# A four-stage gated network on one core: x transposed on TensorE instead of loaded a second time, rows and exponentials on ScalarE, and one list of steps ahead of the routed tiles

## The chip, the cores and the metric

The kernel runs on one core of one Trainium2 chip. The metric is the device time of one execution in microseconds, given as the median of several runs. The engines are called as the profile calls them: PE (TensorE, the matrix engine, with PEld for its weight loads), DVE (VectorE), ACT (ScalarE), POOL (GpSimd) and SP (SyncE, which here only issues transfers, DMAs). Each engine works through its own list of instructions in order, and waits on semaphores where an instruction needs what another engine or a transfer has not finished.

## The reference, cut to what matters

The input x has 4 sequences of 512 tokens with 512 features, 2048 tokens in all. Two layers follow, each an attention part and a feed-forward part, each part added to x through a gate:

```python
x = x + tanh(g_xattn[0]) * L0_xattn(layernorm(x), ctx, desc_router, W_q, b_q, itok)
x = x + tanh(g_ffn[0])   * L0_ffn(layernorm(x), gate_w, bias, experts, shared)
x = x + tanh(g_xattn[1]) * L1_xattn(layernorm(x), ctx, ctx)
x = x + tanh(g_ffn[1])   * L1_ffn(layernorm(x), router_w, experts, shared)

# L0_xattn: 64 sets; each token may see 4 of them (itok), takes the best 2
scores = (ln @ W_q.T + b_q) @ desc_router.T / sqrt(512)
scores = where(mask, scores, -inf)
weights = softmax(top 2 of scores)          # one exp of a difference
out = weights @ ctx                         # 64 rows of 512 per sequence

# L0_ffn: 32 experts, the best 6 for each token, at most 192 tokens per expert
s = sqrt(softplus(h @ gate_w.T))
idx = top 6 of (s + bias);  w = 1.5 * s[idx] / sum(s[idx])
pos = running count of tokens per expert
y = sum of w * down(silu(h @ w_gate) * (h @ w_up)) + shared(h)
```

The change lies in the first two parts: from the load of x up to the point where the first tile of tokens routed to an expert goes through PE. I call this stretch the head. Layer 1 and the routed tiles of layer 0 are not changed.

## The kernel before

**Tiles.** x is kept in SBUF as 16 tiles `xs[t]` of 128 tokens by 512 features. They are handled in four groups of four tiles, `GROUPS[g]`: tile g of each of the four sequences. `lnT[g]` holds a group transposed, features on partitions (128 x 4 x 512). The head works on three parts of the groups for the attention (`PARTS`: group 0, group 1, groups 2 and 3 together; index u) and on two pairs of groups for the feed-forward part (index p: groups 0 and 1, groups 2 and 3).

**Loads.** SP issues them in the order of the code: the descriptor matrix, the four tiles of `w_q`, some small vectors, then per two groups the transposed x from DRAM (`xT`, 1 MB for each group, L133) and the tiles of x (256 KB each, L135). So x is read twice, once in each layout. Then come the weights of the shared expert and of the first two routed experts (L558, L559).

**The head's steps, before.**
- The mask of allowed sets is built by 16 small DVE operations (L296, L298), and `bm` from it (L301). PE multiplies the descriptors with `w_q` (`pm`), ACT and DVE take the row means off (`mrow`), PE transposes the product (`pmt`), and ACT copies it to `mT` (L330).
- `score1(p)`: PE multiplies `mT` with `lnT` of two groups (`pss`, L362), ACT copies (`sT`), PE transposes back (`pst`, L370). The scores of pair 0 serve u = 0 and u = 1.
- `look1(u)`: mean and variance of each x tile on DVE (L354, L355).
- `pick1(u)`: DVE only. It computes the inverse standard deviation by a bit trick and Newton steps (`rsqrt`), scales and masks the scores (L384, L389), finds the best two, and computes the exponential of their difference by a polynomial (`exp_parts`, L235 to L244, 13 operations), which gives the weights `wa`.
- `mix1(u)`: PE transposes `wa` (`pw`), ACT copies (`wT`), PE multiplies with ctx (`po`, L429), DVE adds the result to x and sums the rows (L430); then ACT sums the squares of x less its mean (L440).
- `norm2(p)` turns sums into scale and shift on DVE. `turn2(p)` computes the eight normalised tiles h of the pair on DVE (L470), stores each to `h_dram`, and has it transposed on PE (`transposed`, L256) and copied into `lnT` by ACT (L257). So from here `lnT` holds h.
- `logits2(p)`: router logits by PE (`pl`, L480), copied, transposed (`plt`), copied to `lg`.
- `gate2(p)`: DVE only, from `lg` to the six chosen experts (`sel2`), the running rows (`rows2`) and the weights `wts`, which SP stores beside h (L552). It begins at L505 with a polynomial exponential over 128 x 256.
- `shared0(g, ..., True)` for groups 0 and 1: the shared expert, as matmuls on PE (`pg0s`, `pu0s`, L577), Silu and a scaling on ACT, a product and a clip on POOL (L587, L588), and the down projection with x added (`po0s`, L596, L598).
- At the end the counts: running sums of `rows2` on DVE (L655 to L658), `ptot`, `pcnt` and `ppos` on PE, `counts` stored to `cnt_dram` (L670), the look-up rows `look2` on DVE (L686). Then POOL looks up counts (`found`, L761), DVE turns them into token numbers, POOL fetches the tokens' rows of h (`xb`, L783), and PE starts on the first routed tile (`ptb`, then `gu`, L801).

**What sets the order.** In the head, PE, DVE and ACT keep the order in which the code issues their instructions (`manual_schedule`). The calls are written out one by one after `run` is defined; several steps are Python generators, of which a call of `next` issues one piece. Behind the routed tiles' own loop the order comes from the string `ORDER`, a list of such steps. PSUM is shared: the pool `ps_t` has two buffers (tag "pt") for all transposes, the pool `ps` two for each of the tags "g", "u" and "o". The work pool has nine row buffers (tag "row").

## Time and profile before

| | |
|---|---|
| median of 3 runs | 1096.97 us (1096.78 to 1097.93) |
| the profiled execution's own time | 1097.25 us |
| its span, first to last instruction | 1095.5 us |
| busy in the span: PE | 1004.9 us, 92% |
| DVE | 466.5 us, 43% |
| ACT | 211.5 us, 19% |
| POOL | 376.1 us, 34% |
| mean granted PE clock | 0.961 of full |
| HBM read | 206.16 MB |

The page gives the busy time of each engine and then the span in 40 equal slices of 27.4 us: a digit is the busy share of an engine in tenths, and the row PEclk gives the clock that PE was granted, in tenths of full. A line of the timeline has the start in us, the duration in us, the engine, the line of the code, the operation, the tile written and the tile read, and in brackets how long the engine had been idle before and what released it. A line of the table by stretches has the busy time of each engine in a stretch with the number of its instructions. The duration of a group (x16 and the like) runs from its first start to its last end.

### The profile page before, as it was taken

The page shows a single profiled execution, that of the slowest core. Times are in us where ns is not written, and L with a number is a line of the kernel's source. Part 1 is how long each engine was busy: PE and PEld are TensorE (multiplying, and loading weights), DVE is VectorE, ACT ScalarE, POOL GpSimd, SP SyncE. Part 2 cuts the span into 40 slices and gives each one's busy share as a digit, 9 for nine tenths or more (in the row PEclk, how much of TensorE's full clock was granted, in tenths as well). Part 3 has the DMA queues.
Part 4 walks back from the last instruction along what each step waited for, and adds up shares of the span by engine and source line. Part 5 has one row for each costly group of instructions (what it writes and reads, how often), then busy time and mean ns, then how long its engine had stood idle before and what let it go on. Part 6 is the DMA issues. An engine that isn't in the chain of part 4 may idle for free. (4 is left out here: it accounts for less than half of the span.)

```text
span 1095.5 us, 11070 instructions
## 1 busy us (share of the span) xinstructions
PE 1004.9 (92%) x3334; PEld 491.7 (45%) x3334; DVE 466.5 (43%) x1244; ACT 211.5 (19%) x461; POOL 376.1 (34%) x414
## 2 busy tenths in 40 slices
PE   5569889999999999989779888999999999999998
PEld 2134344444444444434345433655555555544443
DVE  5989946232222232267788452122222222218111
ACT  1144111222222222113344300211111111110000
POOL 2001142234333222177562564445544554300000
PEclk8679999999999999999879899999999999999999
DMA  8622046778788777767463205427453734438111
GB/s 315 246 77 78 7 131 215 250 262 284 254 280 275 279 278 260 253 187 218 147 213 116 59 1 237 164 76 243 129 160 107 257 110 156 157 109 303 39 38 38
DMA packets 88381, 191.94 MB, mean 175 GB/s; under 512 B 24638, under 2 KB 41950, under 8 KB 81920
## 3 DMA queue, kind: packets, MB, share of 16 engines
q1 hardware_dynamic: 59664, 114.46, 29.8%
q0 software_dynamic: 28656, 76.76, 22.9%
q8 instruction: 27, 0.44, 0.2%
q14 instruction: 34, 0.28, 0.1%
HBM read 206.16 MB, written 35.57 MB: 221 GB/s over the span
## 5 line engine op out<-in xcount | busy, mean ns | idle before, releaser
L801 PE MATMUL gu<-wbuf,xbT 128*128 128x512 f32 (+1 forms) x512 | 174.0, 596 | 1.0 <-issue 0.7
L967 POOL DMA_INDIRECT yk<-y_dram,rows_of x76 | 84.1, 1106 | 83.9 <-DVE it0s L590 34.6
L783 POOL DMA_INDIRECT xb<-h_dram,get x48 | 48.0, 1000 | 166.5 <-issue 98.8
L808 DVE SCALAR_TENSOR_TENSOR sgb<-gu,xb,sgb 128x256 f32<-128x256 f32 (+1 forms) x64 | 30.9, 484 | 160.5 <-ACT sgb L806 121.3
L1458 PE MATMUL por<-wbuf,itr 128*128 128x512 f32 (+1 forms) x216 | 98.7, 592 | 0.0
L801 PEld LDWEIGHTS gu<-wbuf,xbT 128*128 128x128 f32 (+1 forms) x512 | 63.1, 163 | 78.0 <-issue 76.9
L1438 PE MATMUL pgr<-wbuf,xrT 128*128 128x352 f32 x288 | 91.6, 461 | 5.4 <-DMA wbuf<-in_wgu_dram,wrow 4.7
L1441 DVE SCALAR_TENSOR_TENSOR sgr<-pur,slots,sgr 128x352 f32<-128x352 f32 x36 | 21.0, 584 | 169.6 <-PE pur L1438 118.3
L826 PE MATMUL pob<-wbuf,itb 128*128 128x512 f32 (+1 forms) x256 | 91.2, 599 | 0.0
L1438 PE MATMUL pur<-wbuf,xrT 128*128 128x352 f32 x288 | 91.1, 459 | 0.0
L1227 PE MATMUL pg<-lnT,wbuf 128*128 128x512 f32 (+1 forms) x224 | 83.6, 561 | 0.1
L1227 PE MATMUL pu<-lnT,wbuf 128*128 128x512 f32 (+1 forms) x224 | 79.6, 532 | 0.0
L1461 POOL DMA_INDIRECT y_dram<-yr,put x36 | 36.8, 1021 | 123.9 <-DVE yr L1460 116.7
L1438 PEld LDWEIGHTS pur<-wbuf,xrT 128*128 128x128 f32 x288 | 54.7, 190 | 30.5
L1243 PE MATMUL po<-wbuf,it 128*128 128x512 f32 x128 | 61.3, 611 | 5.7 <-DVE pick L1322 3.8
L1438 PEld LDWEIGHTS pgr<-wbuf,xrT 128*128 128x128 f32 x288 | 51.9, 190 | 29.4 <-DVE yr L1460 3.8
L1458 PEld LDWEIGHTS por<-wbuf,itr 128*128 128x128 f32 (+1 forms) x216 | 41.0, 190 | 41.9 <-issue 34.9
L761 POOL DMA_INDIRECT found<-cnt_dram,look x48 | 48.5, 1010 | 25.7 <-issue 14.0
L1227 PEld LDWEIGHTS pg<-lnT,wbuf 128*128 128x128 f32 (+1 forms) x224 | 35.2, 184 | 42.7 <-issue 41.4
L1227 PEld LDWEIGHTS pu<-lnT,wbuf 128*128 128x128 f32 (+1 forms) x224 | 35.0, 175 | 40.9 <-issue 38.2
L831 DVE COPY y<-pob 128x512 f32<-128x512 f32 x48 | 33.2, 692 | 43.2 <-PE pob L826 31.6
L1460 DVE TENSOR_TENSOR yr<-por,half_db 128x512 f32<-128x512 f32 x36 | 24.9, 692 | 56.1 <-PE por L1458 50.8
(399 smaller groups left out, 1280.2 us busy)
## 6 DMA issues: line engine op xcount, KB each, us to landing
wbuf<-in_wgu_dram SPq DMA_DIRECT2D x32, 1024.0 KB
wbuf<-in_wd_dram SPq DMA_DIRECT2D x32, 512.0 KB
y_dram<-y SPq DMA_DIRECT2D x48, 256.0 KB
q<-rp SPq DMA_DIRECT2D x256, 32.0 KB
y<-y_dram SPq DMA_DIRECT2D x32, 256.0 KB
lnT<-in_xT_dram SPq DMA_DIRECT2D x4, 1024.0 KB
x<-in_x_dram SPq DMA_DIRECT2D x16, 256.0 KB
h_dram<-h SPq DMA_DIRECT2D x16, 256.0 KB
```

Source lines behind the costliest of these rows:

```text
L761: G.indirect_dma_start(out=found[k][:, j, :], out_offset=None, in_=cnt_dram[:, :], in_offset=bass.IndirectOffsetOnAxis(ap=look2[:, i : i + ...
L783: G.indirect_dma_start(out=rows0[i], out_offset=None, in_=h_dram[:, :], in_offset=bass.IndirectOffsetOnAxis(ap=get2[:, i : i + 1], axis=0) ...
L801: PE.matmul(gu[p_, :], lhsT=xbT[:, c, p_], rhs=weights[e][0][:, c, :], start=(c == 0), stop=(c == DC - 1),)
L808: V.scalar_tensor_tensor(sg[p_, :I0], gu[p_, I0:], xb[p_, D + e : D + e + 1], sg[p_, :I0], ALU.mult, ALU.mult)
L826: PE.matmul(po[p_, :], lhsT=it[:, ic, p_], rhs=weights[e][1][:, ic, :], start=(ic == 0), stop=(ic == I0 // P - 1),)
L831: V.tensor_copy(y, po)
L967: G.indirect_dma_start(out=yk, out_offset=None, in_=y_dram[:, :], in_offset=bass.IndirectOffsetOnAxis(ap=rows_of[:, t, k : k + 1], axis=0) ...
L1227: PE.matmul(p_[m, :n], lhsT=wgu[:, a, c, i], rhs=lnT[g][:, c, k], start=(c == 0), stop=(c == DC - 1))
L1243: PE.matmul(po, lhsT=it[:, ic, k * P : (k + 1) * P], rhs=wd[:, ic, :] if ic < 2 else wd2, start=(ic == 0), stop=(ic == 2),)
L1438: PE.matmul(p_, lhsT=xbT[:, c, :], rhs=wgu[:, a, c, :], start=(c == 0), stop=(c == DC - 1))
L1458: PE.matmul(po, lhsT=it[:ni, ic, :], rhs=wd[:ni, ic, :], start=(ic == 0), stop=(ic == 2))
L1461: d = G.indirect_dma_start(out=y4_dram[:, :], out_offset=bass.IndirectOffsetOnAxis(ap=put4[:, i : i + 1], axis=0), in_=yr, in_offset=None, ...
```

## The change

1. **x is no longer loaded transposed.** The argument `xT` and its four loads are gone. A new step `turn1(g)` has PE transpose each x tile (four 128 x 128 transposes into a buffer of `ps_t`) and ACT copy it into `lnT[g]`, 16 tiles in all.
2. **The mask** is built by POOL: four subtractions of 128 x 256, a product of 128 x 512 and one of 128 x 256, then one comparison with zero on DVE in place of 16 operations.
3. **The exponential in `pick1`** is one ACT activation (Exp), after a maximum on DVE. `gate2` keeps its polynomial.
4. **The h rows** are a step of their own, `rows2_(p)`. For pair 0 ACT computes them (Identity with scale and bias from tiles), for pair 1 DVE as before. `turn2(p)` only transposes.
5. **The counts** become a generator, `count2`, with the same instructions.
6. **One list of steps**, `FIRST_ORDER`, replaces the calls written out. Most steps yield in more places, so that they can be interleaved. A step "j" (`filler`) issues one matmul whose result nobody reads; the list has it twice: on PE it stands once ahead of `pw` of part 1 and once ahead of the last `po0s` of group 1.
7. Following the list, on PE the shared expert's first matmuls stand ahead of `pl` of pair 0, the second half's between the h transposes of pair 1, and group 1's among the `po0s` of group 0. On DVE, `norm2(1)` and seven of the eight h rows of pair 1 stand ahead of `gate2(0)`. On SP, the load of expert 2's first weights stands ahead of the second pair of `wts` stores. The lists of all engines behind the head are the same as before.

The core of the diff:

```diff
+FIRST_ORDER = """
+x1 x0*3 x1 x0 c1 x1*2 c1 c0*2 b0*2 c0*2 f0 x3 x2 x3 c1*2 f0*2 f1 c2 x3 m0*2 x2 x3 x2*2 b1 c2 j f1 m0 c2 f1 m1
+c2 m1 c2 b1 m1 c2*3 n0 h0 f2 h0 t0 h0*3 t0*2 f2 h0 t0*3 f2 m2 h0*2 m2 t0*2 m2*3 n1 h1 e0 h1 g0*2 t1*2 h1*3
+e0*2 h1 t1 h1 t1 r0 t1*3 e0 h1 t1 g1*2 r0 e1 r0 e1 r0 e0 r0 r1*4 o e0 e1 e0*2 e1 o*3 e1*3 r1 o j e1 o*2
+"""
...
-        if g % 2 == 0:
-            for h in range(2):
-                nc.sync.dma_start(out=lnT[g + h], in_=xT[g + h])
...
-    for g in range(TB):
-        V.tensor_scalar(mask[:, g, :], iota_f, itok_f[:, g, 0:1], None, ALU.is_equal)
-        for k in range(1, KSET):
-            V.scalar_tensor_tensor(
-                mask[:, g, :], iota_f, itok_f[:, g, k : k + 1], mask[:, g, :], ALU.is_equal, ALU.max
-            )
+    hit = chain[:, 1:5, :].rearrange("p a n -> p (a n)").rearrange("p (k g n) -> p k g n", k=KSET, n=N)
+    for k in range(KSET):
+        G.tensor_tensor(
+            hit[:, k], iota_f[:, None, :].to_broadcast([P, TB, N]),
+            itok_f[:, :, k : k + 1].to_broadcast([P, TB, N]), ALU.subtract,
+        )
+    G.tensor_tensor(hit[:, 0:2], hit[:, 0:2], hit[:, 2:4], ALU.mult)
+    G.tensor_tensor(mask, hit[:, 0], hit[:, 1], ALU.mult)
+    V.tensor_scalar(mask, mask, 0.0, None, ALU.is_equal)
...
+    def turn1(g):
+        for t in GROUPS[g]:
+            transposed(cols(t), xs[t], f"ptx{t}")
+            yield
...
-        exp_parts(r, d, m, q)
+        V.tensor_scalar(d, d, -87.0, None, ALU.max)
+        A.activation(r, d, AF.Exp)
+        yield
...
-    def turn2(p):
+    def rows2_(p):
         rs, nb = norms2[p]
         for j, t in enumerate(tiles2(p)):
-            h = work.tile([P, D], F32, name=f"h{t}", tag="row", bufs=NROW)
-            V.tensor_scalar(h, xs[t], rs[:, j : j + 1], nb[:, j : j + 1], ALU.mult, ALU.add)
+            h = hs[t] = work.tile([P, D], F32, name=f"h{t}", tag="row", bufs=NROW)
+            if p == 0:
+                A.activation(h, xs[t], AF.Identity, bias=nb[:, j : j + 1], scale=rs[:, j : j + 1])
+            else:
+                V.tensor_scalar(h, xs[t], rs[:, j : j + 1], nb[:, j : j + 1], ALU.mult, ALU.add)
             nc.sync.dma_start(out=h_dram[t * P : (t + 1) * P, :D], in_=h)
-            transposed(cols(t), h, f"pth{t}")
+            yield
+
+    def turn2(p):
+        for t in tiles2(p):
+            transposed(cols(t), hs.pop(t), f"pth{t}")
+            yield
...
+    def filler():
+        while True:
+            pj = ps_t.tile([P, DC, P], F32, name="pj", tag="pt")
+            PE.matmul(pj.rearrange("p c t -> p (c t)"), lhsT=ones, rhs=ctx_sb[:, 0, :], start=True, stop=True)
+            yield
...
+    ws0 = load_w0(0, wsgu0, wsd0)
+    does = {"o": count2()}
+    for p in range(2):
+        does |= {f"b{p}": score1(p), f"n{p}": norm2(p), f"h{p}": rows2_(p), f"t{p}": turn2(p), f"g{p}": logits2(p)}
+        does |= {f"r{p}": gate2(p), f"e{p}": shared0(p, *ws0, True)}
+        does |= {f"x{2 * p + a}": turn1(2 * p + a) for a in range(2)}
+    for u in range(len(PARTS)):
+        does |= {f"c{u}": look1(u), f"f{u}": pick1(u), f"m{u}": mix1(u)}
+    in_steps(FIRST_ORDER, does)
```

In the list a letter names a step and the digit its group, pair or part: x transposes of x, c statistics, b scores, f picks, m mixing, n norms, h rows, t transposes of h, g logits, r gate, e shared expert, o counts, j filler; "*3" issues three pieces.

## The prediction

> **What bounds the kernel now.** The page comes first: the sum of the busy shares, then the slices of 27.4 us.
>
> ```profile
> span 1095.5 us, 11070 instructions
> ...
> PE   5569889999999999989779888999999999999998
> ...
> DVE  5989946232222232267788452122222222218111
> ...
> PEclk8679999999999999999879899999999999999999
> ```
>
> PE is full nearly everywhere but in the first three slices, where DVE is full instead. The table by stretches splits there (columns: length, busy us of PE, PEld, DVE, ACT, POOL, then granted clock, DMA share, GB/s).
>
> ```profile
> 16.00:82.00 66.00, 38.73 (x136) 18.08 (x133) 56.98 (x239) 16.43 (x38) 0.00 (x0) 0.74 0.53 203
> 82.00:134.00 52.00, 45.48 (x137) 20.71 (x135) 48.50 (x159) 17.29 (x33) 8.77 (x8) 0.99 0.13 44
> 154.00:1095.00 941.00, 894.73 (x2988) 438.67 (x2988) 341.99 (x784) 172.10 (x380) 353.85 (x364) 0.98 0.55 181
> ```
>
> From 16 to 134 us DVE works 105.5 of 118 us, nearly all there is once gaps of 0.03 us between instructions are taken off; PE has slack and a clock of 0.74 in the first half. After 154 PE works 895 of 941 us, and the built instruction lists of all five engines are alike there in both kernels. So the change is worth what it moves the first routed tile (ptb, at 154.02), and that passes to the end. The timeline gives the stations on the way (start, duration, engine, line).
>
> ```profile
> 22.73 0.42 DVE L384 TENSOR_TENSOR s<-pst,rs_a 128x256 f32<-128x256 f32 x1 [0.72 <-PE pst L370]
> ...
> 82.26 0.42 DVE L505 SCALAR_TENSOR_TENSOR chain<-lg 128x256 f32<-128x256 f32 x1
> ...
> 133.22 0.69 DVE L658 TENSOR_TENSOR rows<-rows,upto 128x512 f32<-128x512 f32 x1
> ...
> 134.05 1.94 PE L661 MATMUL ptot<-rows,ones 128*128 128x480 f32 x2 [4.91 <-DVE rows L658]
> ...
> 143.54 1.64 POOL L761 DMA_INDIRECT found<-cnt_dram,look  x1 [11.35 <-DVE chain L704]
> ```
>
> The reader should see four stages: first scores (22.73), router logits of pair 0 taken up by DVE (82.26), running counts (end 133.85), first look-up (143.54). I carry the change through these, in the order of the built lists, with durations of this execution.
>
> **First scores: later.** Gone are four loads of 1 MB of xT. The first scores didn't wait for them long: pss started at 15.11, 0.05 after mT. In their place stand eight tile transposes and copies, behind a later mT. The mask moves from 16 DVE operations (4.65 us, from 6.89) to six on POOL: 128x256 lies between POOL's 0.44 us for 128x128 and its 1.30 for 128x512, so 0.70 each for five and 1.25 for one, with memsets between them 5.6 us from 6.8, end 12.4. DVE's list then has two mask operations, and behind them the mean of the score matrix, which PE needs: pmt starts at 13.85 instead of 12.56, and ends at 15.98. x tiles should be there: bytes flow at 400 GB/s from 9.1, and the first two groups with ctx are 2.5 MB, 6.3 us. Eight transposes follow, 0.89 us a tile at half clock (the eight h tiles from 61.73 took 6.86) and 0.66 at full clock, where ACT's 0.59 copy sets the pace.
>
> Here a rule speaks against the change. The rows:
>
> ```profile
> 60.00:64.00 4.00, 2.27 (x11) 2.08 (x12) 3.79 (x13) 0.88 (x2) 0.00 (x0) 0.50 0.40 148
> 64.00:67.00 3.00, 3.00 (x15) 2.35 (x13) 2.93 (x21) 2.03 (x4) 0.00 (x0) 0.50 1.02 383
> 67.00:68.00 1.00, 1.00 (x7) 0.76 (x6) 0.97 (x9) 0.61 (x2) 0.00 (x0) 0.66 0.92 346
> ```
>
> PE did only transposes from 61.73, and was granted full clock at about 67.7, 5.9 us after their start. The Trainium skill (TensorE: Matmul & The Clock Gate, Part 4: PE-mode transpose) says that transposes don't count as PE activity and full clock doesn't engage for them. By that rule all eight tiles run cold (7.1 us, 1.0 more than below), and the first 5 us of the score group too. That group took 6.24 us at 15.11, some 4.4 of them at half clock, so it is 4.1 at full clock; with 5 us at half clock it is 6.6, 2.5 more. Scores come 3.5 us later still, and the forecast below would be 1097.8. I go by the row: full clock about 5 us into dense work (the rises at 19.5, 36.9, 50.6 and 67.7 came 3.3 to 6.9 after), here at 19. Then: four tiles at 0.89 to about 19.4, four at 0.66 to 22.1, last copy 22.75, pss 4.1 to 26.9, sT 0.6, pst 0.7: DVE takes the scores at 28.2, 5.5 us later than now.
>
> **DVE's picks: that is won back.** Each pick loses 13 small operations (25.64 to 28.23, 2.6 us) for one maximum (0.2) and an Exp on ACT. No row shows this Exp; the nearest is the 128x2 activation at 9.46, 0.20 us, so 0.3 with both hand-overs: 2.1 us off, three times. The built list has no further table load for it. Bounds 0.2 to 0.6 each. Exp stands between copies on ACT, but those end 0.7 us earlier. Laid out: first pick 5.3 + two statistics 1.6 to 35.1; second scores 3.1, statistics and adds of four x tiles 3.55, rest of the second pick with statistics and the row means to 48.3; a wait of 0.6 for pw, wT, po; adds and statistics 6.2 and 0.5 of waiting for ACT's squares to 55.6; norm2 2.2 to 57.85; third pick 9.9: wa is there at 67.75, now 73.2. The second four-tile transposes of x use PE's idle time; their single free ps_t buffer (pst holds the other) costs them 1.4 us a tile, which nobody waits for. The two filler matmuls (0.45 us each) fall into waits of PE, for wa of the second pick and for xb at the end, where it rests 2.3 us now. The h rows of pair 0 leave DVE (3.74 us); on ACT they are priced by Square with a bias, 0.71 (no row has both scale and bias by pointer; by the Trainium skill, ScalarE: Activation LUTs, What ACT_TABLE_LOAD costs, each pointer adds 93 ns, so an estimate of 0.80). Five of them and three copies end at 63.5, before the third Exp at 64.8, so they cost nothing at either price; were the cover of 1.3 us gone, each row would cost its own 0.7.
>
> **Then DVE waits for others.** wa to x adds: pw, wT, po at half clock, 2.65 us, adds from 70.4. PE has rested since about 51 and then transposed with gaps, so I take it cold until about 74.5 (72.8 to 76.2): adds end 78.05. Squares on ACT end at 81.0, and nothing is queued on DVE for these 3 us, where it now does part of gate2. norm2 2.2, seven rows 3.2: 86.5. Meanwhile PE, after po (76.6), does eight shared matmuls (3.5 + 3.5) ahead of the logits: pl 4.1, lT, plt, lg 1.6: 89.25. So gate2(0) begins at 89.25, with norm2(1) and seven rows behind it, where now (82.26) they are still ahead.
>
> **Counts and look-up.** From there DVE is full again: first part of gate2 5.65, the last row 0.46, the rest 15.5 (95.20 to 110.71), gate2(1) to the counts 23.14 now, of which 2.0 are lost to POOL. The row for this loss:
>
> ```profile
> 88.32 1.30 POOL L587 TENSOR_TENSOR it0s<-it0s,sg0s 128x512 f32<-128x512 f32 x1 [80.70 <-DVE rs_b L214]
> 88.51 1.12 DVE L216 TENSOR_TENSOR rw_b<-rw_b,n 128x8 f32<-128x8 f32 x1
> ```
>
> A DVE operation of 0.17 us took 1.12 and ended with POOL's. The four POOL pairs now cost DVE 1.4, 0, 1.3 and 0.7; three meet it in the new stretch, taken at 0.7 each (bounds 0 and 1.4). Sum: 89.25 + 5.65 + 0.46 + 15.5 + 21.15 + 2.1 = 134.1, against 133.85. PE's list from plt (88.8): two h tiles 1.35, eight shared matmuls 7.0, six tiles with the last copy behind ACT's Silu 5.75, pl to plt 5.35, eight matmuls 7.0, two po0s 5.15, eight 7.0, two 5.15, so it ends at 132.4. Now it rested from 129.1 to 134.05 in this place and lost its clock at 132.5 (3.4 us after). A rest of 1.7 us keeps it: ptot, pcnt cost 2.7 instead of 5.4 (134.05 to 139.5), counts are stored at 137.8 and land 3.2 later (140.31 to 143.5 now), while the look-up rows, 4.4 us behind wts (136.2), are there at 140.7. First look-up at 140.9: 2.6 us earlier. The step in SP's list, weights ahead of the second pair of wts, waits for matmuls that end at 127 and holds nothing up: the two wts stores, ready only at 136.2, and counts follow it.
>
> **Sum.** The profiled execution is 1097.25 us with a span of 1095.5, 0.3 above the median of the runs. 1096.97 - 2.6 = 1094.3. A difference under 0.2% (2.2 us) is about what can't be told from none.
>
> **Rivals.**
> - *PE warm earlier*: the four h transposes between 60.9 and 64.8 lift the clock, po and the shared matmuls start 2.6 us earlier, and DVE's wait at 86.5 goes: 1091.7. For: they keep PE 94% busy for nearly 4 us. Against: stretches of 84 and 86% (30.1 to 33.5, 12.6 to 16.0) didn't lift it, and this one is short.
> - *The waits eat it all*: Exp at 0.5, mask at 0.8 us an operation, 1.2 lost per POOL pair: 0.6 + 0.6 + 1.5 = 2.7 more, so 1097.0. PE's list moves by the first 1.2 too, its rest before the counts is then 3.2 us, and the clock just holds. The change then does what it says, but removed DVE work has only turned into waits for PE and ACT. That x is loaded once saves nothing in any case.
> - *Slower*: the clock falls before the counts. It fell 3.4 us after PE's last matmul (129.1 to 132.5). If DVE alone is later by over 1.7 us, PE rests for more than 3.4, and ptot and pcnt run at half clock, 2.7 us more: from there on 1094.3 + 1.7 + 2.7 = 1098.7, and a us more for each us of delay; its middle is 1099.2. For: exactly this happens now. Against: it needs the delay first, from nearly full losses to all three POOL pairs.
>
> **Chances.** The forecast has 0.50, with 1092.8 to 1096.2 as its own range (clock in the middle ±0.8, POOL ±1.4); about two thirds of it is over 0.2%. Warm earlier 0.17, waits 0.17, slower 0.16. Faster 0.33 + 0.17 + 0.02 = 0.52; slower 0.16; within 0.2% the remaining 0.32. The range for 8 in 10 goes from the warm case with a POOL pair saved to the slower one: 1090.0 to 1099.2.
>
> **What would show it.** Right: pst's reader on DVE near 28, wa of the third pick near 68, gate2's first operation near 89 behind a wait for lg, no clock loss before ptot, found near 141, the 940 us behind unchanged. Wrong: scores before 25 or after 31; gate2 starting without a wait; ptot at clock 0.5; routed tiles whose PE time differs.

## The result, and the profile after

The changed kernel takes 1100.22 us (median of 20 runs, 1096.29 to 1105.04); the kernel before, run beside it, takes 1096.62 us (median of 20). The ratio is 1.0036, with a 95% interval of 1.0022 to 1.0051: 0.36%, or 3.9 us, slower. (On some of the chips used below an execution is now and then in a slower state; ratios and intervals leave these out.) The forecast was 1094.3 us, so both its direction and its range were wrong. The profiled execution took 1100.35 us, with a span of 1098.2 us.

Times of one and the same kernel spread over 8 us and more from run to run, and the kernel before had medians of 1094 to 1105 us on the chips used below. Each kernel has one profiled execution. The places at which a step happens within the head repeat to 1 or 2 us from one profile to the next, and the distance between two steps that no edit touches mostly to 0.2 us. So the readings below rest on these, and the times are given with their intervals.

The page of the changed kernel: span, two of the engines' busy tenths in slices of 27.4 us, and the clock.

```profile
span 1098.2 us, 11181 instructions
...
PE   6679789999999999998869996999999899999998
...
DVE  3868955323223232277788441122222222218111
...
PEclk8869989999999999999889898999999999999999
```

DVE's first four slices are emptier than before (3868 against 5989). PE's clock is higher in the second slice (8 tenths against 6) and lower in the third (6 against 7). The head has less DVE work, as intended. The table by stretches says how much (columns: length, busy us of PE, PEld, DVE, ACT, POOL, then granted clock, DMA share, GB/s):

```profile
16.00:82.00 66.00, 46.72 (x190) 24.95 (x191) 48.35 (x199) 33.80 (x73) 0.00 (x0) 0.77 0.36 140
82.00:134.00 52.00, 46.50 (x149) 19.96 (x147) 47.23 (x148) 14.56 (x26) 7.56 (x7) 1.00 0.18 64
154.00:1095.00 941.00, 894.78 (x2992) 439.43 (x2990) 343.84 (x799) 172.59 (x381) 355.28 (x366) 0.98 0.56 181
```

Between 16 and 82 us DVE works 48.4 us instead of 57.0: 8.6 us are gone. ACT does 33.8 instead of 16.4. Behind 154 us PE's busy time is the same to 0.05 us. So the difference is to be looked for in the head and at the first routed tile, and the timeline shows where (start, duration, engine, line, operation, tiles, and in brackets the idle time before and its releaser):

```profile
27.93 0.42 DVE L403 TENSOR_TENSOR s<-pst,rs_a 128x256 f32<-128x256 f32 x1 [3.04 <-PE pst L388]
49.34 0.75 DVE L453 SCALAR_TENSOR_TENSOR x<-po,a,x 128x512 f32<-128x512 f32 x1 [2.14 <-PE po L452]
72.25 0.75 DVE L453 SCALAR_TENSOR_TENSOR x<-po,a,x 128x512 f32<-128x512 f32 x1 [4.02 <-PE po L452]
82.11 0.17 DVE L483 TENSOR_SCALAR n<-n 128x8 f32<-128x8 f32 x1 [3.05 <-ACT sq L463]
89.16 0.42 DVE L542 SCALAR_TENSOR_TENSOR chain<-lg 128x256 f32<-128x256 f32 x1 [1.54 <-ACT lg L526]
136.13 0.69 DVE L687 TENSOR_TENSOR rows<-rows,upto 128x512 f32<-128x512 f32 x1
136.87 1.97 PE L690 MATMUL ptot<-rows,ones 128*128 128x480 f32 x2 [5.79 <-DVE rows L687]
146.35 1.71 POOL L796 DMA_INDIRECT found<-cnt_dram,look  x1 [11.26 <-DVE chain L728]
157.08 0.63 PE L262 MATMUL ptb<-ident,xb 128*128 128x128 f32 x4 [1.67 <-DMA xb<-h_dram,get]
158.38 5.40 PE L836 MATMUL gu<-wbuf,xbT 128*128 128x512 f32 x8 [0.67 <-ACT xbT L263]
```

The last of these lines in the kernel before:

```profile
155.35 3.70 PE L801 MATMUL gu<-wbuf,xbT 128*128 128x512 f32 x8 [0.68 <-issue]
```

The reader should see three things. First, DVE now waits in five places, 13.8 us in these lines (3.04 + 2.14 + 4.02 + 3.05 + 1.54), where the kernel before waited 4.0 us in two of them (0.72 for the first scores, 3.28 for `po` of the third part). The forecast had a wait at each of the five, though not always of its size. Second, the counts end at 136.82 instead of 133.91, and behind them `ptot` runs at half clock, as it did before; the first look-up is 2.8 us later than before. Third, which the forecast did not have at all, the first routed matmuls (`gu`) take 5.40 us where they took 3.70 before. They end at 163.78 instead of 159.05, 4.7 us later; the span ends 2.7 us later. Where the routed part wins 2.0 us back is not shown.

### The profile page after: what moved, and what is told of

It is laid out like the page before. It is cut to its first block, busy times and chain, and to the rows that moved or that the text cites. A ratio compares the mean times of both kernels' runs of the same rounds, so it can differ in the third digit from the quotient of the medians.

```text
span 1098.2 us, 11181 instructions
## 1 busy us (share of the span) xinstructions
PE 1012.9 (92%) x3402; PEld 498.6 (45%) x3402; DVE 454.1 (41%) x1185; ACT 225.6 (21%) x488; POOL 379.6 (35%) x420
## 5 line engine op out<-in xcount | busy, mean ns | idle before, releaser
L841 ACT ACTIVATE sgb<-gu 128x256 f32<-128x256 f32 x48 | 18.4, 384 | 150.7 <-PE gu L836 150.7
```

## The experiments

This table is the summary: starts in us, except the end of the counts and the durations of `ptot` (its larger group) and `gu`. The ratio is to the kernel before on the same chip.

| kernel | scores | gate2(0) | counts end | ptot | look-up | ptb | gu | ratio |
|---|---|---|---|---|---|---|---|---|
| before | 22.73 | 82.26 | 133.91 | 1.94 | 143.54 | 154.02 | 3.70 | 1 |
| changed | 27.93 | 89.16 | 136.82 | 1.97 | 146.35 | 157.08 | 5.40 | 1.0036 |
| pool_out | 28.82 | 89.14 | 131.95 | 1.04 | 138.98 | 149.30 | 3.70 | 0.9969 |
| fill | 29.12 | 89.22 | 136.87 | 1.07 | 143.82 | 154.14 | 3.70 | 0.9990 |
| g0_first | 29.12 | 89.67 | 135.61 | 1.07 | 142.74 | 153.21 | 3.70 | 0.9958 |
| x_load | 28.57 | 88.89 | 136.53 | 1.97 | 146.02 | 156.60 | 5.40 | 1.0032 |
| x_load2 | 24.58 | 86.84 | 134.49 | 1.97 | 144.13 | 154.88 | 5.40 | 1.0001 |
| mask_dve | 27.96 | 89.57 | 137.21 | 1.97 | 146.81 | 157.33 | 3.70 | 1.0120 |
| rows_dve | 28.83 | 93.60 | 141.2 | 1.97 | 150.93 | 161.16 | 3.70 | 1.0132 |
| pool_out_before | 22.64 | 81.82 | 130.10 | 1.04 | 140.47 | 151.40 | 6.33 | 1.0011 |
| fill_before | 23.30 | 82.48 | 134.12 | 1.04 | 145.09 | 156.11 | 5.97 | 1.0027 |
| act_store | 22.62 | 82.15 | 133.81 | 1.04 | 144.08 | 155.24 | 6.68 | 1.0008 |
| all | 22.55 | 83.92 | 129.86 | 0.97 | 137.87 | 149.15 | 3.70 | 0.9964 |
| warm | 23.69 | 83.34 | 129.32 | 0.97 | 137.28 | 148.57 | 3.70 | 0.9960 |

### POOL's pairs taken out (pool_out)

```diff
             if early:
                 A.mul(it[:, ic, :], pu, gf[:, 0:1])
-                G.tensor_tensor(it[:, ic, :], it[:, ic, :], sg, ALU.mult)
-                G.tensor_scalar(it[:, ic, :], it[:, ic, :], lim[:, 0:1], lim[:, 1:2], ALU.min, ALU.max)
```

> The changed kernel without POOL's product and clip in the shared expert of groups 0 and 1: this leaves out the product of Silu and up, and the clip, for these two groups. Theory P (POOL's pairs hold DVE, 4.8 us in all, and that delay also drops PE's clock ahead of the counts): DVE's running counts end at 132.0 instead of 136.82, PE's rest ahead of ptot falls from 5.8 to about 1 us, ptot and pcnt run at full clock (2.7 us less), first look-up at 138.9 instead of 146.35, time about 1092. Rival C (the clock at the counts is lost for another reason, POOL costs DVE 4.8 us all the same): counts at 132.0, look-up at 141.5, time about 1095.5. Rival N (the long DVE operations there are long for a reason of their own): counts stay near 136.8, time near 1100.

Theory P, to 0.1 us at the counts (131.95) and at the look-up (138.98). The ratio is 0.9969 (0.9951 to 0.9987); against the changed kernel's 1.0036 that is 0.67%, about 7.3 us. The changed kernel's rows at two of the four places, POOL and DVE side by side:

```profile
91.85 3.66 DVE L248 SCALAR_TENSOR_TENSOR chain<-chain 128x256 f32<-128x256 f32 x5
...
93.03 1.30 POOL L624 TENSOR_TENSOR it0s<-it0s,sg0s 128x512 f32<-128x512 f32 x1 [80.97 <-ACT it0s L623]
...
101.59 1.38 POOL L624 TENSOR_TENSOR it0s<-it0s,sg0s 128x512 f32<-128x512 f32 x1 [6.35 <-ACT it0s L623]
...
101.87 1.38 DVE L553 SCALAR_TENSOR_TENSOR chain<-lg,chain 128x256 f32<-128x256 f32 x1
103.29 0.75 DVE L220 TENSOR_SCALAR chain<-chain 128x256 int32<-128x256 int32 x1
```

And the same DVE lines without POOL's pairs, with `ptot` behind them:

```profile
91.83 2.26 DVE L248 SCALAR_TENSOR_TENSOR chain<-chain 128x256 f32<-128x256 f32 x5
...
100.45 0.43 DVE L553 SCALAR_TENSOR_TENSOR chain<-lg,chain 128x256 f32<-128x256 f32 x1
100.91 0.29 DVE L220 TENSOR_SCALAR chain<-chain 128x256 int32<-128x256 int32 x1
...
132.10 1.04 PE L688 MATMUL ptot<-rows,ones 128*128 128x480 f32 x2 [1.06 <-DVE rows L685]
```

Five operations take 2.26 us instead of 3.66, one takes 0.43 instead of 1.38, one 0.29 instead of 0.75. From gate2's start to the end of the counts it is 42.81 us instead of 47.66: the four pairs cost DVE 4.85 us, where the forecast took 2.1. And with PE's rest ahead of `ptot` at 1.06 us instead of 5.79, `ptot` takes 1.04 us instead of 1.97. Rivals C and N fall.

### Fillers ahead of the counts (fill)

```diff
-... o e0 e1 e0*2 e1 o*3 e1*3 r1 o j e1 o*2
+... o e0 e1 e0*2 e1 j*6 o*3 e1*3 r1 o j e1 o*2
```

> The changed kernel with six more filler matmuls (0.86 us each at full clock) on PE ahead of ptot, in PE's rest of 5.8 us. Theory P (the clock ahead of the counts is lost by this rest alone): counts on DVE end at 136.8 as they do now, ptot and pcnt take 2.7 us less, look-up at 143.7 instead of 146.35, time about 1097.5. Rival C (the counts come late for the look-up whatever PE's clock, for instance by the stores of the weights ahead of them): look-up stays at 146 or above, time 1100 to 1101.

Right again: counts on DVE unmoved (136.87), look-up at 143.82. PE's timeline:

```profile
130.96 5.31 PE L653 MATMUL pj<-ctx_sb,ones 128*128 128x512 f32 x12
136.91 1.07 PE L690 MATMUL ptot<-rows,ones 128*128 128x480 f32 x2 [0.65 <-DVE rows L687]
```

Six useless matmuls in place of a rest make what follows 2.5 us shorter. The clock of the changed kernel in that rest (same columns as the stretches above) shows what they prevent:

```profile
132.00:134.00 2.00, 0.00 (x0) 0.00 (x0) 1.93 (x18) 0.78 (x2) 1.14 (x1) 1.00 0.00 0
134.00:136.00 2.00, 0.00 (x0) 0.00 (x0) 1.74 (x6) 0.00 (x0) 0.99 (x2) 0.86 0.00 0
136.00:138.00 2.00, 1.13 (x2) 0.67 (x3) 1.88 (x6) 0.00 (x0) 0.00 (x0) 0.50 0.00 0
```

The clock falls within the stretch from 134 to 136, at 135.4 if it went in one step from 1 to 0.5 (a mean of 0.86 means 0.56 us at half). That is 4.4 us after PE's last matmul (131.07). The gain in time is larger than the 2.5 us: the ratio is 0.9990 (0.9971 to 1.0009), 0.46% or 5 us under the changed kernel. The first `gu`, too, ran at full clock (3.70), so the routed part began 2.9 + 1.7 = 4.6 us earlier.

### The logits ahead of the shared matmuls (g0_first)

```diff
-... m2*3 n1 h1 e0 h1 g0*2 t1*2 h1*3 ...
+... m2*3 n1 h1 g0*2 e0 h1 t1*2 h1*3 ...
```

> The changed kernel with the router logits of pair 0 ahead of the first eight shared matmuls on PE. Theory P: lg is there at about 82, gate2 of pair 0 starts right behind the h rows, at 87.6 instead of 89.16; what POOL's pairs hit on DVE changes with it (4.8 us may become 3.5 to 5.5); counts at 135.3, PE's rest 4.2 us, so the clock falls late or not at all: look-up at 142 to 144.8, time 1096 to 1098.7. Rival W: the 1.5 us are taken by a later wait of DVE, counts at 136.8, time near 1100.

The lowest ratio of the single edits, though its interval overlaps that of pool_out: 0.9958 (0.9938 to 0.9978), 0.78% or 8.5 us under the changed kernel. This run's steps up to norm2(1) are 2.1 us late (84.23 instead of 82.11; nothing there was edited, but its clock rose at 76.46 instead of 73.99), and still gate2 starts at 89.67. DVE's timeline:

```profile
86.46 3.29 DVE L499 TENSOR_SCALAR h<-x,rs_b,n 128x512 f32<-128x512 f32 x7
89.67 0.41 DVE L542 SCALAR_TENSOR_TENSOR chain<-lg 128x256 f32<-128x256 f32 x1
...
92.34 2.26 DVE L248 SCALAR_TENSOR_TENSOR chain<-chain 128x256 f32<-128x256 f32 x5
...
96.09 1.75 DVE L546 RECIPROCAL chain<-chain 128x256 f32<-128x256 f32 x1
```

Three effects add up. The wait for `lg` is gone: from norm2(1) to gate2 it is 5.44 us instead of 7.05. The shared expert comes later, so POOL's first pair (96.44 here, to 98.81) now mostly meets a reciprocal, which keeps its 1.75 us, and not the five operations of L248, which keep their 2.26; and the fourth pair (from 136.20) now falls behind the counts. From gate2 to their end it is 45.94 us instead of 47.66. And PE's list ends at 134.4 instead of 131.07, so that it rests 1.24 us ahead of `ptot` and keeps its clock there and at `gu`. The expectation had the direction and a look-up of 142 to 144.8 (142.74); its 1096 to 1098.7 us counted neither the effect on POOL's pairs nor the two clock losses saved in full. These places account for 5.6 of the 8.5 us (`ptb` 3.9 us earlier, `gu` 1.7 shorter). Against the kernel before, the first routed tile comes only 0.8 us earlier, but the time is 4.6 us less (2.4 to 6.8). The 2.1 us by which this one execution was late may be a part of that; the rest is not shown.

### x loaded transposed again (x_load and x_load2)

```diff
     for g in range(B):
+        if g % 2 == 0:
+            for h in range(2):
+                nc.sync.dma_start(out=lnT[g + h], in_=xT[g + h])
...
         for t in GROUPS[g]:
-            transposed(cols(t), xs[t], f"ptx{t}")
             yield
```

> The changed kernel with x loaded a second time, transposed, in place of the 16 tile transposes and their copies; all else stays. Theory P with its view of the head (DVE sets the pace from its first scores on, and these wait for the transposes of x): scores on DVE at 24.1 instead of 27.93, wa of the third pick near 64.5 instead of 68.2, gate2 of pair 0 near 85.4 instead of 89.16, counts at 133 instead of 136.82, PE's list ends earlier by as much, so the clock falls as before: look-up near 142.5, time about 1096.4. Rival W (what comes earlier is taken by later waits of DVE): scores at 24.1, but gate2 of pair 0 still after 88 and the look-up after 145.5, time 1099 to 1100.

A miss that taught something: the scores come at 28.57 instead of the 24.1 of both theories, and all else stays (look-up 146.02, ratio 1.0032). The line that explains it:

```profile
21.39 0.69 DVE L367 BATCH_NORM_STATS2 s<-x 128x6 f32<-128x512 f32 x1 [3.02 <-DMA x<-in_x_dram]
```

The list puts the statistics of two tiles of group 1 first on DVE. With 2 MB of transposed x ahead of them in SP's list, those tiles come late: DVE stands at 21.39 for a transfer, with the statistics of group 0 queued behind. One part of the change had been fitted to the other. So the next kernel also turns the order of the statistics:

```diff
-x1 x0*3 x1 x0 c1 x1*2 c1 c0*2 b0*2 c0*2 f0 x3 x2 x3 c1*2 f0*2 f1 c2 ...
+x1 x0*3 x1 x0 c0*2 x1*2 c0*2 b0*2 c1 f0 x3 x2 x3 c1 f0 c1 f0 c1 f1 c2 ...
```

> The changed kernel with x loaded transposed again, and now with the statistics of group 0 ahead of those of group 1 in DVE's list (one of group 1 ahead of the first scores, three behind), because the loads bring group 1's tiles late. Theory P: scores on DVE at 24.6 instead of 27.93, second scores at 33.8 instead of 36.6, gate2 of pair 0 near 85.8 instead of 89.16, counts near 133.5, look-up near 143, time near 1097. Rival W (the first scores are not on the path that sets the end, the waits behind them take any gain): gate2 of pair 0 at 88.5 or later, time as the changed kernel.

Scores at 24.58 and second scores at 33.81, as expected. Then the gain of 2.8 us shrinks a little: gate2 at 86.84, counts at 134.49, look-up at 144.13, each 2.2 to 2.3 us ahead of the changed kernel, with the same falls of the clock behind them. So theory P stands with a smaller number: the transposes of x on PE, placed ahead of the first scores, cost 2.2 us of the head in this pair of profiles. The size is not certain: norm2(1) begins at 79.80 here, and at 82.11 in the changed kernel, but the runs without an edit ahead of it also differ (82.10 in pool_out, 82.16 in fill, 84.23 in g0_first). The ratio, 1.0001 (0.9976 to 1.0026), is consistent with that, but its interval is too wide to show it.

### The mask and the h rows back on DVE (mask_dve, rows_dve)

```diff
-    for k in range(KSET):
-        G.tensor_tensor(
...
+    for g in range(TB):
+        V.tensor_scalar(mask[:, g, :], iota_f, itok_f[:, g, 0:1], None, ALU.is_equal)
...
```

> The changed kernel with the mask built on DVE by 16 operations as before; all else stays. Theory P: the mean of the score matrix no longer stands behind POOL, pmt starts at 12.6 instead of 13.4, the x transposes 0.8 to 1.3 us earlier, scores on DVE at 26.7 to 27.2 instead of 27.93, and everything behind as much earlier (gate2 of pair 0 at 88.2, look-up at 145.4): moving the mask to POOL cost up to 1 us. Rival W (the gain is taken by the wait for po of part 1, or by x tiles that are not there earlier): gate2 of pair 0 at 89 or later.

By its stations this is rival W: scores at 27.96, gate2 at 89.57. But the run is not a clean comparison. `itok`, from which the mask is built, came later: DVE's CAST of it starts at 7.41 instead of 6.53. From there to the first `pmt` it is 5.95 us with the mask on DVE, against 6.85 in the changed kernel and 6.86 in fill and g0_first. So the mask on POOL does cost 0.9 us at `pmt`, as theory P has it. Whether these would reach gate2 is not shown; fill speaks against it, where `itok` came at 7.20, the scores 1.2 us later than in the changed kernel, and gate2 still at 89.22. The time (1.0120, 1.0041 to 1.0199, from three runs) is above the changed kernel's without a station in the head that says why; that stays open.

```diff
-            if p == 0:
-                A.activation(h, xs[t], AF.Identity, bias=nb[:, j : j + 1], scale=rs[:, j : j + 1])
-            else:
+            if True:
                 V.tensor_scalar(h, xs[t], rs[:, j : j + 1], nb[:, j : j + 1], ALU.mult, ALU.add)
```

> The changed kernel with the eight h rows of pair 0 back on DVE (0.47 us each there); all else stays. Theory P (DVE up to the third wa is on the path that sets the end, so this part of the change saves what it takes off DVE): the six rows ahead of the third wa bring it to 71.0 instead of 68.2, gate2 of pair 0 to 92 instead of 89.16, counts 139.6, look-up 149, time 2.5 to 3 us above the changed kernel. Rival W (the saving on DVE only turned into a wait for PE and ACT): wa later, but gate2 of pair 0 within 0.7 us of 89.16 and the look-up within 0.7 us of 146.35.

Theory P: gate2 at 93.60 and the look-up at 150.93, 4.4 and 4.6 us later than in the changed kernel (0.9 of it was there at the scores already). This part of the change does save: about 3.5 us, most of the 3.7 that it takes off DVE. The ratio (1.0132, four runs, 1.0072 to 1.0193) agrees in sign, but mask_dve's is as high without such a cause, so it carries no weight.

### The same two cuts in the kernel before (pool_out_before, fill_before, act_store)

The first leaves out the same two POOL lines as pool_out, the second puts five matmuls of 128x512 ahead of `ptot`.

> The kernel before, without POOL's product and clip in the shared expert of groups 0 and 1 (left out: the product of Silu and up, and the clip, for these groups). Theory P: here the pairs hold DVE for 3.4 us, so the counts end at 130.5 instead of 133.85; PE's rest ahead of ptot falls from 4.9 to 1.4 us, so its clock holds: look-up at 137.4 instead of 143.54, some 6 us off the time, against 7.3 us in the changed kernel. Of the 2.8 us by which the changed kernel's look-up is late, then, 1.2 are left. Rival (POOL's pairs cost only the changed kernel, because of where its list puts them): counts within 1 us of 133.85, time within 2 us of the kernel before.

> The kernel before with five filler matmuls (0.86 us each) on PE ahead of ptot, in its rest of 4.9 us. Theory P: the clock holds at ptot and pcnt as it does in the changed kernel with fillers: look-up at 140.9 to 141.3 instead of 143.54, time 2 to 3 us below the kernel before. Then the fall of the clock at the counts is common to both kernels, and the changed kernel's loss is the later counts and the second fall, at the first routed tile. Rival: no gain here (look-up at 143 or later), and the clock's fall is the changed kernel's own.

The counts came as theory P had them (130.10, and 134.12 with `ptot` at 1.04 us), so the pairs cost DVE 3.4 us before (gate2 to the end of the counts 48.28 instead of 51.65), against 4.85 after, and the fall of the clock at the counts is common to both kernels. But neither kernel became faster (1.0011, 0.9987 to 1.0035; 1.0027, 1.0000 to 1.0055). Their gain is lost twice. PE's timeline of pool_out_before:

```profile
130.25 1.04 PE L659 MATMUL ptot<-rows,ones 128*128 128x480 f32 x2 [1.54 <-DVE rows L656]
...
151.40 0.99 PE L256 MATMUL ptb<-ident,xb 128*128 128x128 f32 x4 [4.98 <-DMA xb<-h_dram,get]
153.07 6.33 PE L799 MATMUL gu<-wbuf,xbT 128*128 128x512 f32 x8 [0.68 <-ACT xbT L257]
```

PE is done with its list sooner at full clock, so it rests 4.98 us ahead of the first routed tile instead of 2.33, and there the clock falls: `gu` takes 6.33 us. The second loss is the store of the counts. In both kernels the look-up comes 6.5 us after the store was issued (133.95 to 140.47, 138.62 to 145.09), where it is 3.2 us in the kernel before (140.31 to 143.54) and 3.2 to 3.4 in the changed kernel and all that come from it. SP's own lines of fill_before, with the look-up's line from POOL:

```profile
136.91 1.62 SPq L558 DMA_DIRECT2D wbuf<-in_wgu_dram  x1
138.62 0.39 SPq L673 DMA_DIRECT2D cnt_dram<-counts  x1
...
145.09 1.27 POOL L764 DMA_INDIRECT found<-cnt_dram,look  x1 [12.67 <-DMA cnt_dram<-counts]
```

A load of 1 MB was issued 1.7 us ahead of the store, and 1.1 us in pool_out_before. In the kernel before it goes 3.6 us ahead (136.69 and 140.31), in the changed kernel 17.2 us (125.95 and 143.19). Is it the queue that holds the store, or the 16 DMA engines? The next kernel has the store issued by ACT's queue:

```diff
-    nc.sync.dma_start(out=cnt_dram[: NT * E0, :].rearrange("(k p) t -> p k t", p=P), in_=counts)
+    nc.scalar.dma_start(out=cnt_dram[: NT * E0, :].rearrange("(k p) t -> p k t", p=P), in_=counts)
```

> The kernel before with five fillers ahead of ptot, as in the run with these fillers, and with the counts' store issued by ACT's queue instead of SP's. In that run the store was issued at 138.62, 1.7 us behind a load of expert 2's weights, and the look-up came at 145.09, 6.5 us after it, where it is 3.2 us in the kernels whose load went earlier. Theory Q (the store waits in its queue behind the load): with another queue the look-up comes at 141.8, time some 3 us below the kernel before unless the clock falls at the first routed tile. Rival B (all 16 DMA engines are busy with the load, whatever the queue): look-up at 144 to 145 again.

Rival B: the store was issued at 137.66, 1.1 us behind the load, and the look-up came at 144.08, 6.4 us later. Another queue did not help. (The Trainium skill says the same, in DMA: Bandwidth & Descriptors, Issuing engines are not separate DMA queues: transfers run on the same 16 engines whichever engine started them.)

### Put together (all, warm)

```diff
-x1 x0*3 x1 x0 c1 x1*2 c1 c0*2 b0*2 c0*2 f0 x3 x2 x3 c1*2 f0*2 f1 c2 ...
+x1 x0*3 x1 x0 c0*2 x1*2 c0*2 b0*2 f0 x3 x2 x3 c1 f0 c1 f0 c1*2 f1 c2 ...
-... n1 h1 e0 h1 g0*2 t1*2 ... e0*2 e1 o*3 e1*3 r1 o j e1 o*2
+... n1 h1 g0*2 e0 h1 t1*2 ... e0*2 e1 j*3 o*3 e1*3 r1 o j e1 j*2 o*2
```

with the loads of xT and the mask on DVE as in the diffs above.

> The changed kernel with what the study points to put together: x loaded transposed with the statistics of group 0 first, the mask on DVE, the logits of pair 0 ahead of the shared matmuls, three fillers ahead of ptot and two ahead of the first routed tile. Its exponentials, the h rows of pair 0 on ACT and the rest of the list stay. Theory P: scores at 23.3, gate2 of pair 0 at 83 to 85, counts at 131 to 133, clock held through the counts and the first routed tile, look-up at 138.5 to 140.5, time 1088 to 1091, under both kernels. Rival W: look-up at 142.7 as with the logits moved alone, time near 1092.

Faster than both: 0.9964 (0.9937 to 0.9990). Gate2 at 83.92, counts at 129.86, look-up at 137.87 (0.6 below the expected 138.5), first routed tile at 149.15, 4.9 us ahead of the kernel before, with the clock held at both places. Its median was 1099.57 us beside 1104.33 for the kernel before on that chip, so the expected 1088 to 1091 us were missed with the chip's level; the difference is 4 us. The head is shorter than with the logits alone, but the two ratios (0.9964, 0.9958) can't be told apart.

The last kernel has one more filler among the h transposes of pair 0 (`t0*2 j t0` in place of `t0*3`):

> The version put together (x loaded transposed, statistics of group 0 first, mask on DVE, logits of pair 0 first, three fillers ahead of ptot and two ahead of the first routed tile) with one more filler between the h transposes of pair 0, in a gap of PE of 1.2 us. Theory P: PE is then dense from 57.7 on and has full clock when pw of the third pick starts, so DVE's wait from wa to the x adds is 2.9 to 3.3 us instead of 4.02, and gate2 of pair 0 starts 0.5 to 1.5 us earlier than the 83.92 without the filler; look-up at 136.5 to 137.5. Rival (one filler doesn't lift the clock there): the wait stays at 4.0 and pw is later by up to 0.6; look-up at 138 to 138.5.

The wait came down as theory P had it:

```profile
68.93 0.75 DVE L451 SCALAR_TENSOR_TENSOR x<-po,a,x 128x512 f32<-128x512 f32 x1 [2.61 <-PE po L450]
```

But the cause was another. PE's lines and the clock there:

```profile
61.62 1.56 PE L265 MATMUL pth<-ident,h 128*128 128x128 f32 x8 [0.31 <-ACT lnT L266]
64.79 1.13 PE L651 MATMUL pj<-ctx_sb,ones 128*128 128x512 f32 x2 [1.61 <-ACT lnT L266]
```

```profile
60.00:62.00 2.00, 1.69 (x9) 1.29 (x8) 1.93 (x16) 2.00 (x4) 0.00 (x0) 0.50 0.71 261
62.00:64.00 2.00, 1.18 (x8) 0.94 (x6) 1.66 (x15) 0.69 (x3) 0.00 (x0) 0.84 0.37 144
64.00:66.00 2.00, 1.21 (x5) 0.68 (x6) 1.90 (x5) 1.23 (x3) 0.00 (x0) 1.00 0.34 131
```

The clock was up between 62 and 64, before the filler started at 64.79. The h transposes, begun at 57.23 and nearly without gaps from 59.37 on, had raised it in this run and not in the others; the last section says what set this run apart. The filler may have kept the clock up, though: with it PE was busy for 53% of the 3.41 us behind the rise (62.63 to 66.04). Without it, by an estimate from these lines (0.55 us of the transposes begun at 61.62, 0.60 of the next four), it would be 34%, and the last section shows falls behind such stretches. What the run does show is the size: with a warm PE the wait from the third wa to the x adds is 2.61 us instead of 4.02, and gate2 comes 0.6 us earlier although the scores were 1.1 us later. The ratio is 0.9960 (0.9934 to 0.9987), as without the filler.

## Why the prediction was wrong

**Right.** The changed kernel was forecast station by station, and up to gate2 it goes as forecast: scores 28.2 (27.93), third wa 67.75 (68.23), gate2(0) 89.25 (89.16). The Exp on ACT took its 0.20 us with 0.27 of waiting for DVE, the h rows 0.80. Squares of pair 1 left DVE idle for 3.05 us, as said. The stretch behind 154 did not change. The weighing of row against rule came out for the row: PE had only x transposes from 15.87 on (behind the matmuls of `pmt`), and full clock came at about 19.4:

```profile
18.00:19.00 1.00, 1.00 (x7) 0.86 (x6) 0.96 (x3) 0.65 (x2) 0.00 (x0) 0.50 1.06 389
19.00:20.00 1.00, 1.00 (x7) 0.65 (x6) 0.96 (x3) 0.79 (x2) 0.00 (x0) 0.81 1.06 389
20.00:21.00 1.00, 0.86 (x8) 0.64 (x7) 0.93 (x4) 0.79 (x3) 0.00 (x0) 1.00 1.05 378
```

The score group behind them took 4.39 us (forecast 4.1; 6.6 by the rule that the prediction quotes from the Trainium skill, TensorE: Matmul & The Clock Gate, Part 4: PE-mode transpose, that transposes don't count as activity). How soon the clock rose was luck in part: in four runs with the same list up to there (pool_out, fill, g0_first, rows_dve) it rose at 21.2 to 22.3, with transposes begun 0.4 to 0.8 us later, and the scores came at 28.8 to 29.1.

**Wrong, the step that decided: the sum for the counts.** It took three POOL pairs at 0.7 us each, 2.1 in all, between bounds of 0 and 1.4. Four pairs met the stretch and cost 4.85 us. The error is 2.7 us, and that is the whole of the counts' delay: 134.1 forecast, 136.82 measured. Two mistakes lie in it. The first piece of gate2 was priced at 5.65 us, from the profile before, in which no pair met it, and was not charged with one: it took 1.40 more. And the other three, at 0.7 each, took 1.41, 1.39 and 0.65 (line by line against pool_out), 1.35 more than the 2.1. 0.7 was the middle between bounds, where the row of before already told which end applies: a pair that met two-input operations cost 1.4, one that met a reciprocal cost nothing:

```profile
95.18 1.43 POOL L587 TENSOR_TENSOR it0s<-it0s,sg0s 128x512 f32<-128x512 f32 x1 [4.70 <-ACT it0s L586]
...
95.52 1.75 DVE L509 RECIPROCAL chain<-chain 128x256 f32<-128x256 f32 x1
97.31 0.46 DVE L510 TENSOR_TENSOR chain<-chain 128x256 f32<-128x256 f32 x1
```

The Trainium skill has this as a rule (SBUF — State Buffer, Who interferes with whom): a DVE instruction with two inputs in SBUF, or in its two-port fast mode, and a POOL instruction that reads SBUF exclude one another for a whole instruction. The traces agree: lengthened were tensor_tensor and scalar_tensor_tensor with both inputs in SBUF, even of 128x8, and tensor_scalar (0.29 to 0.75); not the reciprocal, and not the match_replace of the picks. Gate2's long chains are of the first kind, so each pair that lands in them should have had the 1.4; only the last, at the picks, had the 0.7.

**Wrong as its consequence: the clock at the counts.** The forecast had PE rest 1.7 us and keep its clock. The rest was 5.79: 2.7 more from the delay, and 1.3 more because PE's list ended at 131.07 instead of 132.4. `ptot` and `pcnt` ran cold for 2.7 us more. This is the rival called *Slower*, with its mechanism and its price. It asked for a delay of over 1.7 us "from nearly full losses to all three POOL pairs". At the delay that came it would give 1094.3 + 2.7 + 2.7 = 1099.7, and 1100.22 was measured. Its chance of 0.16 was too low, since the losses were no accident but followed from the kind of operation that gate2 is made of.

**Not in any case: the clock at the first routed tile.** `gu` took 5.40 us instead of 3.70, 1.7 us more. The clock:

```profile
158.00:160.00 2.00, 1.61 (x3) 0.82 (x4) 0.08 (x2) 0.33 (x1) 1.70 (x2) 0.83 0.98 377
```

By the working used for 135.4 above it fell at 159.32, within `gu`. The length of the rests doesn't explain it: PE rested 1.67 us ahead of `ptb` and 0.67 behind it, but in the kernel before 2.33 and 0.68, and there the clock held. What differs is how the rests lie to the points, 3.41 us apart, at which the clock can change (last section). In the 3.41 us that end at 159.32 PE was busy for 46%. In the kernel before such a point, at 153.02, cuts the rest in two, and the 3.41 us behind it have 51%. The sum of the three, 1094.3 + 2.7 + 2.7 + 1.7 = 1101.4, is 1.2 above the result. The mask_dve run had the same list at this place and the same kind of rests (1.47 and 0.67), with PE busy for 53% of such a stretch, and kept its clock; x_load and x_load2 (47% each) lost it. So this fall is not certain from one execution to the next.

**Off, without effect.** The wait from the third wa to the x adds was 4.02 instead of 2.65, since `pw` and `wT` alone took 1.9 and the first two `po` were cold; the wait for po of part 1 was 2.14 instead of 0.6. Both vanish in the waits behind them, since gate2 started by PE's logits. A filler was priced at 0.45 us and takes 0.86 at full clock. The forecast's terms for PE's list up to the counts add up to 132.55, not 132.4, and the rise that it puts at 19.5 in the kernel before was at 19.90. And the step in SP's list was rightly priced at nothing for the forecast's path, but it is not worth nothing: it takes 1 MB out of the way of the counts' store, 3.3 us, as soon as nothing else holds the look-up.

**So where did the removed DVE work go?** Into waits, as the rival *The waits eat it all* has it: 8.6 us less DVE work up to 82 us, and gate2 6.9 us later, with norm2(1) and seven h rows (5.5 us) done ahead of it. What could be won back stood in PE's list (logits behind the shared matmuls, 1.5 us; transposes of x ahead of the first scores, 2.2 us) and in the clock (2.5 + 1.7 us). The ACT rows were a true saving of about 3.5 us.

## What to carry to other kernels

When DVE work is taken off a stretch, go on to ask what the engine will meet at its new times: POOL's instructions cost it 1.4 us a pair in chains of two-input operations and nothing as long as they meet a reciprocal or the picks, so the price of an overlap is read from the kind of operation it falls on, not from an average. And where PE waits for several us ahead of a short, urgent group of matmuls, look at how busy PE is over the whole stretch of 3.4 us, short rests included: two rests of 1.67 and 0.67 us were enough at the first routed tile, where both fell into one such stretch. Here both kernels paid 2.5 us at the counts, and six useless matmuls removed that, but only where PE then had no long rest at the next place too. A list that was fitted to one arrangement of loads has to be fitted anew when the loads change.

## What was not expected of the hardware

- The clock's fall moves on rather than goes away. In the kernel before, keeping it at the counts (`ptot` 1.04 instead of 1.94 us) made PE's list end sooner, PE rested 5 to 5.7 us ahead of the first routed tile, and `gu` took 6.0 to 6.7 us instead of 3.70 in three runs of three.
- The clock changed only at points of a fixed grid. Worked out like the 135.4 above, from stretches of half a us, its changes in the kernel before lie at 13.07, 19.90, 26.72, 36.96, 43.79, 50.62, 54.03, 67.68, 132.54 and 139.36, and each is a whole multiple of 3.413 us behind the first, to 0.01 us. In all 14 profiles, up to 170 us, the changes lie on such a grid, with another start in each (12.55 in the changed kernel, 11.43 in warm). The Trainium skill (TensorE: Matmul & The Clock Gate, Part 1: The HAM clock gate) describes a free-running window of 3413 ns, and the traces agree.
- What counted was how busy PE was between two points of the grid. In these 14 profiles, from 10 to 170 us, every fall followed a stretch with PE busy for at most 49%, every rise one with at least 86%. At full clock every stretch under 45% was followed by a fall, those of 45 to 49% went both ways. Some of 86% and more did not raise the clock, four of them at 100% with the small `pmt` matmuls ahead of x transposes. Stretches filled with 128x128 transposes alone raised it all seven times (64.27 to 67.68 before, 15.96 to 19.38 after). In warm the stretch from 59.22 to 62.63 was busy for 86%, with h transposes alone; in the kernel put together, with the same list so far, the grid lay otherwise, and its stretch from 59.93 to 63.34 had 63%. So the same list can be warm in one execution and cold in the next.
- A store of 256 KB behind a load of 1 MB issued 1.1 to 1.7 us earlier reached its reader 6.4 to 6.5 us after its issue, instead of 3.2, on SP's queue and on ACT's alike.
